# Attention with relative positions on one Trainium2 core: another DRAM layout for the position terms of the scores

## The chip, the core and the metric

The kernel runs on one core of a Trainium2 chip. The core has a matrix engine (TensorE; PE in the profile, with its weight loads shown as PEld), a vector engine (DVE), an activation engine (ACT), a general engine (POOL) and a synchronisation engine (SP), which here issues nearly all DMA transfers. Sixteen DMA engines move the data between DRAM (HBM) and the on-chip memory SBUF. The metric is the device time of one execution in microseconds (us); lower is better.

## What is computed

The reference is one transformer block over 16 sequences of 512 tokens with 256 channels, all in float32: a modulated layer normalisation, attention with 16 heads of 16 channels and relative positions, a second modulated normalisation, and a layer of 8 experts of which two count for each token. What matters here is the attention's scores:

```python
scores = jnp.einsum('bhqd,bhkd->bhqk', q, k)
dist_idx = pos_l - pos_r + M - 1
pos_emb = dist_emb[dist_idx]
rel_q = jnp.einsum('bhld,lrd->bhlr', q, pos_emb)
rel_k = jnp.einsum('bhrd,lrd->bhlr', k, pos_emb)
scores = (scores + rel_q + rel_k) / jnp.sqrt(jnp.asarray(D, scores.dtype))
probs = jax.nn.softmax(scores, axis=-1)
```

`rel_q + rel_k`, called the terms below, is a number for each batch, head, query position l and key position r: 16 x 16 x 512 x 512 values, 268 MB in all. The kernel works them out with (batch, head) on the 128 partitions, but the scores need l on the partitions. So the terms go through DRAM once: written in one arrangement, read back in the other. The change is about how they lie there.

## The kernel before, in words

**Tiles of the terms.** The 16 sequences are taken in two halves `s` of 8; 8 sequences times 16 heads are 128 rows, one for each partition. The 512 query positions are cut into four ranges `lb` of 128 and each of these into two of 64 (`lh`); the key positions into four ranges `rb` of 128 (`RK`). A block `n` (0 to 63) is one (s, lb, rb, lh): 128 rows x 64 l x 128 r, held in one of two buffers `two[n % 2]`. `q_set(n, g)` (line 156) makes 16 of its 64 l for all r with matrix products copied out by ACT (lines 165 and 175); `k_set(n, g)` (line 177) adds the second term for 32 of its 128 r and all 64 l, with products added in by DVE (lines 186 and 195). `store(n, g)` (line 199) writes 16 of the 64 l to DRAM: 1 MB. So all four `k_set` of a block must be done before its first store.

**In DRAM.** There are eight tensors `rel_d`, one for each (s, lb) (line 115). Each holds 128 rows (batch, head), 128 l and 512 r: 32 MB. Eight blocks, hence 32 stores, fill one.

**Reading back.** The main loop takes a unit `u` (0 to 63) = (s, lb, one sequence): 128 query positions of one sequence, 16 heads, in four groups `g` of four heads. `load_scores(u, g)` (line 577) brings the terms of four heads into a tile `st` of 128 l x 4 heads x 512 r, 1 MB; four such tiles exist (line 550). `content(u, g)` (line 637) multiplies queries and keys (line 644), and DVE adds the loaded terms and takes the maximum, one instruction for each head `t` (line 650). `exps` exponentiates (line 660), `turn` transposes the result on PE (line 669, out through lines 672 and 674), `context` multiplies with the values (line 687). The output projection, the second normalisation and the experts (lines 698 to 860) follow for the unit before.

**Two stages.** First a prologue: `prepare(b)` makes queries, keys and values of all 16 sequences and puts them in DRAM; `stationary(s)` loads them again as `raw` tiles, reorders and transposes them into the operands `e` of the blocks, and stores these (`e_d`); `blocks(n)` makes the first ten blocks (`LEAD = 10`, line 398), merged with the rest by hand. Then constants such as the experts' weights `we_sb` are loaded (line 558), and the main loop runs. It is written out by hand: each unit has 16 slots, and the table of lines 868 to 912 puts every step into a slot. With q0 = 16u + 4g:

- `load_scores(u, g)` in slot q0 - 12, `content(u, g)` in q0 - 4, `exps` in q0 - 2 and q0 - 1, `turn(u, g, t)` in q0 + t, `context(u, g)` in q0 + 5. The tile that a load fills is the one that `turn` of the group four before has last read, in slot q0 - 13.
- the four stores of block u + 10 in slots 16u + 28, 30, 32 and 34; its last `k_set` in slot 16u + 27.
- the other loads of a unit between them: keys `k` (line 590), queries `qs` (601), values `vu` (621), and `hbu`, `xu`, `gt`, `gf` for the later steps (628 to 634); the operands `qe` and `ke` of the next block (153); one store of the result (859).

The units 54 to 63 make no more blocks, since all 64 are done.

**Order.** Each engine runs its instructions in the order in which the program lists them. Nearly all DMAs stand in SP's one list: an SP instruction that waits holds back every DMA behind it. The framework gives the DMAs completion semaphores and the waits. The eight blocks of an `rel_d` tensor are all stored before the first unit that reads it; the last of these stores stands two slots ahead of that load.

Of the kernel before, what the change touches and what calls it, by code (L numbers as in the profile page):

```python
# [8 lines left out]
F32 = mybir.dt.float32  # L9
# [7 lines left out]
P = 128  # L17
E = 256
S = 512
# [10 lines left out]
RK = 128  # L30
# [4 lines left out]
def adaln_attention_moe_kernel(  # L35
# [34 lines left out]
    nc = tc.nc  # L70
    NB = x.shape[0]
    NL = S // P
# [8 lines left out]
    dram = ctx.enter_context(tc.tile_pool(name="dram", bufs=1, space=DRAM))  # L81
# [30 lines left out]
        for s in range(2)  # L112
    }

    rel_d = [dram.tile([P, P, S], F32, tag=f"rel_{n}", name=f"rel_d{n}") for n in range(8)]

    ps = ctx.enter_context(tc.tile_pool(name="ps", bufs=7, space=PSUM))
    ps_c = ctx.enter_context(tc.tile_pool(name="ps_c", bufs=1, space=PSUM))
# [7 lines left out]
    class Rel:  # L126
# [72 lines left out]
        def store(self, n, g):  # L199

            s, lb, rb, lh = self.at(n)
            l0 = lh * LQ + 16 * g
            nc.sync.dma_start(
                out=rel_d[s * 4 + lb][:, l0 : l0 + 16, rb * RK : (rb + 1) * RK],
                in_=self.two[n % 2][:, 16 * g : 16 * g + 16, :],
            )

# [3 lines left out]
    with ExitStack() as pro:  # L211
# [205 lines left out]
        with tc.tile_pool(name="setup", bufs=1) as su:  # L417
# [7 lines left out]
            for name, w in (("wq", wq), ("wk", wk), ("wv", wv)):  # L425
                nc.scalar.dma_start(
                    out=w_sb[name], in_=w.rearrange("(kc p) n -> p kc n", p=P)
# [78 lines left out]
            for t in range(4):  # L506
                for i in range(2):
                    rows = slice(32 * t + 16 * i, 32 * t + 16 * i + 16)
                    nc.sync.dma_start(
                        out=t_f[rows, i, i : 2 * S], in_=ext[:, 0 : 2 * S - i]  # L510
                    )
                    nc.sync.dma_start(
                        out=t_r[rows, i, i : 2 * S - 1], in_=rev[:, 0 : 2 * S - 1 - i]
# [4 lines left out]
                out=m8, in_=m8, compare_op=ALU.is_ge, fill=0.0,  # L518
# [3 lines left out]
                out=m8, in_=m8, compare_op=ALU.is_ge, fill=0.0,  # L522
# [7 lines left out]
        for cc in range(NE):  # L530
            for pa in range(2):
                for t in range(4):
                    row = cc * P + t * 32 + pa * D
                    nc.sync.dma_start(
                        out=wo_sb[pa * 64 + t * D : pa * 64 + (t + 1) * D, cc, :],
                        in_=wo[row : row + D, :],
# [34 lines left out]
    def place(u):  # L571
        s, lb, bb = u // 32, u % 32 // 8, u % 8
        return s, lb, bb, s * HB + bb
# [3 lines left out]
    def load_scores(u, g):  # L577

        s, lb, bb, b = place(u)
        h0 = bb * H + (g // 2) * 8 + g % 2  # L580
        st = sp.tile([P, 4, S], F32, tag="s", name=f"s_{u}_{g}")
        nc.sync.dma_start(
            out=st, in_=rel_d[s * 4 + lb][h0 : h0 + 7 : 2].rearrange("h l r -> l h r")
        )
        units[u]["s", g] = st

    def load_k(u, cc):
# [280 lines left out]
    for u in range(NP):  # L868
        z = 16 * u
        for g in range(4):  # L870
            q0 = z + 4 * g
            at(q0 - 12, 0, load_scores, u, g)
            at(q0 - 4, 5, content, u, g)
            at(q0 - 2, 7, exps, u, g, (0, 1))
            at(q0 - 1, 7, exps, u, g, (2, 3))
            for t in range(4):
                at(q0 + t, 3, turn, u, g, t, t > 0)
            at(q0 + 5, 4, context, u, g)
# [23 lines left out]
        n = u + LEAD  # L902
# [62 lines left out]
```

## Time and profile before

| | |
|---|---|
| Time, three runs | 2971.85, 2974.68, 2978.81 us (median 2974.68) |
| Profiled execution, its own time | 2971.56 us |
| Its span, first to last instruction | 2969.8 us |
| Mean granted TensorE clock | 0.971 |
| Terms written, DMAs | 256 of 1 MB, median 8.5 us from issue to landing |
| Terms read, DMAs | 256 of 1 MB, median 7.8 us from issue to landing |
| DRAM read, written in all | 462 MB, 328 MB |

The profile is a page of one execution and a trace that can be asked further. Its line of 40 slices shows each engine's busy share in tenths; each slice is 74 us, so the prologue is about the first six and a half, and the units without blocks are the last four. The chain of waits follows the end of the program back from releaser to releaser. The windows give busy time, granted clock and DMA share for any stretch. Columns are named where lines are shown.

### The profile page before, as it was taken

Reading aid. Unit: us, or ns where it says so; the run is one execution under the profiler, and the core shown is the slowest. Engines: PE = TensorE matmul, PEld = TensorE weight load, DVE = VectorE, ACT = ScalarE, POOL = GpSimd, SP = SyncE. Lnnn points to the kernel's source line nnn. Section 1 sums busy time; section 2 is a strip of 40 time slices with the busy share of each in tenths; the row PEclk is TensorE's granted clock in tenths of the full one; section 3 lists DMA queues with packets and bytes.
Section 4 is the critical chain, followed back from the end, with each engine's and each line's share of the span. In section 5 each row is a group of like instructions: output and inputs, shape, how many; then the busy total and the mean of one; then the engine's idle time right before and its main releaser. Section 6 shows DMA issues by size and latency. Waiting matters only on the chain.

```text
span 2969.8 us, 75984 instructions
## 1 busy us (share of the span) xinstructions
PE 2815.0 (95%) x30186; PEld 1845.8 (62%) x30186; DVE 1984.0 (67%) x5396; ACT 1933.7 (65%) x3682; POOL 629.8 (21%) x863
## 2 busy tenths in 40 slices
PE   8889864999999999999999999999999999999997
PEld 5556552666666666666666666666666666666564
DVE  5446542777777777777767777677777767776664
ACT  2344433777776777777677677777767777767774
POOL 1000000121222222122222212222222222222333
PEclk9889866999999999999999999999999999999999
DMA  6879997798988889988888998888898888898661
GB/s 191 302 260 319 298 302 259 229 290 268 287 269 271 280 283 293 280 272 281 272 271 277 287 281 274 268 283 277 281 295 268 286 273 272 272 280 279 211 232 54
DMA packets 855346, 796.46 MB, mean 268 GB/s; under 512 B 25545, under 2 KB 649409, under 8 KB 854737
## 3 DMA queue, kind: packets, MB, share of 16 engines
q1 hardware_dynamic: 854032, 790.03, 84.3%
q8 instruction: 240, 3.93, 0.5%
q10 hardware_dynamic: 960, 1.57, 0.2%
q14 instruction: 114, 0.93, 0.1%
HBM read 462.20 MB, written 328.25 MB: 266 GB/s over the span
## 4 chain that ended last, share of the span: by engine, by line
PE 79%; POOL 2%; DMA 1%; DVE 1%; SPq 1%; issue 1%; ACT 1%; POOLq 0%; ACTq 0%; DVEq 0%
PE pt L669 18%; PE fpy L830 14%; PE pq L165 13%; PE qk L644 12%; PE pc L687 8%; PE pk L186 8%; PE ph L735 2%; PE fpl L791 1%; PE pcl L702 1%; POOL qm L614 1%; DMA vu<-v_d 1%; PE fpt L778 1%; PE fpb L821 0%; PE pct L719 0%; POOL rstd L101 0%
## 5 line engine op out<-in xcount | busy, mean ns | idle before, releaser
L175 ACT COPY r<-pq 128x512 f32<-128x512 f32 x1024 | 525.4, 603 | 385.8 <-PE pq L165 368.9
L195 DVE TENSOR_TENSOR r<-pk,r 128x512 f32<-128x512 f32 x1024 | 635.0, 683 | 192.8 <-PE pk L186 187.3
L660 ACT ACTIVATE s<-s,mx 128x512 f32<-128x512 f32 x1024 | 691.6, 735 | 50.2 <-DVE mx L654 47.2
L650 DVE CUSTOM_DVE_ANT_0 s<-qk,s 128x512 f32<-128x512 f32 x1024 | 644.0, 685 | 39.2 <-PE qk L644 36.7
L669 PE MATMUL pt<-ident,s 128*128 128x128 f32 x4096 | 652.0, 283 | 10.7 <-ACT s L660 10.3
L669 PEld LDWEIGHTS pt<-ident,s 128*128 128x128 f32 x4096 | 451.0, 142 | 289.3 <-issue 77.7
L672 ACT COPY pT<-pt 128x512 f32<-128x512 f32 x768 | 459.5, 598 | 252.1 <-PE pt L669 250.4
L851 POOL TENSOR_TENSOR ye<-ye,ye 128x256 f32<-128x256 f32 x192 | 140.6, 732 | 1633.0 <-ACT ye L845 1627.5
L830 PE MATMUL fpy<-we_sb,fhT 128*128 128x512 f32 x1024 | 483.4, 595 | 0.0
L165 PE MATMUL pq<-t_r,qe 32*128 32x256 f32 x4096 | 467.1, 417 | 4.0 <-DMA qe<-eq_d 2.9
L644 PE MATMUL qk<-k,qm 32*128 32x512 f32 x2048 | 388.9, 644 | 28.0 <-POOL qm L614 28.0
L186 PEld LDWEIGHTS pk<-t_f,ke 32*128 32x128 f32 x8192 | 268.8, 190 | 189.1 <-ACT pT L672 157.7
L841 DVE SCALAR_TENSOR_TENSOR fy<-fpy,fmask,fy 128x256 f32<-128x256 f32 x256 | 123.8, 483 | 384.6 <-PE fpy L830 375.6
L165 PEld LDWEIGHTS pq<-t_r,qe 32*128 32x128 f32 x4096 | 283.3, 186 | 143.1 <-DVE mx L650 67.8
L186 PE MATMUL pk<-t_f,ke 32*128 32x128 f32 x8192 | 321.2, 288 | 7.2 <-DVE r L195 3.4
L687 PE MATMUL pc<-pT,vu 128*32 128x128 f32 x8192 | 278.2, 277 | 0.0
L830 PEld LDWEIGHTS fpy<-we_sb,fhT 128*128 128x128 f32 x1024 | 175.4, 191 | 124.9 <-issue 124.9
L687 PEld LDWEIGHTS pc<-pT,vu 128*32 128x32 f32 x8192 | 209.2, 110 | 43.5 <-issue 42.9
L644 PEld LDWEIGHTS qk<-k,qm 32*128 32x128 f32 x2048 | 141.5, 183 | 104.6 <-DVE r L195 47.3
L674 DVE COPY pT<-pt 128x512 f32<-128x512 f32 x256 | 174.5, 682 | 24.9 <-PE pt L669 20.3
L101 POOL TENSOR_TENSOR rstd<-rstd,mhalf 128x1 f32<-128x1 f32 (+1 forms) x144 | 88.0, 611 | 438.5 <-DVE rstd L100 434.9
L845 ACT ACTIVATE ye<-fpy,fmask 128x256 f32<-128x256 f32 x256 | 127.5, 498 | 45.2 <-DVE fy L841 45.1
(111 smaller groups left out, 2175.6 us busy)
## 6 DMA issues: line engine op xcount, KB each, us to landing
rel_d<-r SPq DMA_DIRECT2D x256, 1024.0 KB, 8.5
s<-rel_d SPq DMA_DIRECT2D x256, 1024.0 KB, 7.8
vu<-v_d SPq DMA_DIRECT2D x64, 576.0 KB, 7.7
ke<-ek_d SPq DMA_DIRECT2D x128, 256.0 KB, 7.1
k<-k_d SPq DMA_DIRECT2D x128, 256.0 KB, 6.5
gt<-gates_d SPq DMA_DIRECT2D x64, 256.0 KB, 4.7
v_d<-v SPq DMA_DIRECT2D x16, 576.0 KB, 6.4
xt<-in_x SPq DMA_DIRECT2D x16, 512.0 KB, 6.1
```

Of the source, the lines that this page charges most:

```text
L165: nc.tensor.matmul(bs[t][:, a * 256 : (a + 1) * 256], e[32 * t : 32 * t + 32, (g % 2) * 2 + a, :], t_r[32 * t : 32 * t + 32, :, m0 : m0 + RK],
L175: nc.scalar.copy(dst[:, t], bs[t].rearrange("p (a c) -> p a c", a=2))
L186: nc.tensor.matmul(bs[t][:, a * 128 : (a + 1) * 128], e[32 * t : 32 * t + 32, a, :], t_f[32 * t : 32 * t + 32, :, m0 : m0 + LQ], start=Tru ...
L195: nc.vector.tensor_tensor(dst, bs[t].rearrange("p (r l) -> p l r", r=8), dst, ALU.add)
L644: nc.tensor.matmul(bs[t], t_["q"][rows, pa, cc, :], t_["k", cc][rows, :], start=True, stop=True)
L650: nc.vector.tensor_tensor_reduce(st[:, t, :], bs[t], st[:, t, :], 0.25, -3.0e38, ALU.add, ALU.max, mx[:, t : t + 1],)
L660: nc.scalar.activation(t_["s", g][:, t, :], t_["s", g][:, t, :], AF.Exp, bias=t_["m", g][:, t : t + 1])
L669: nc.tensor.transpose(pt[:, cols], t_["s", g][:, t, cols], ident)
L672: nc.scalar.copy(pT, pt)
L674: nc.vector.tensor_copy(pT, pt)
L687: nc.tensor.matmul(pc[32 * t : 32 * t + 32, g, :], t_["v"][:, rb, h * VW : h * VW + 32], pTs[t][:, rb * P : (rb + 1) * P], start=(rb == 0) ...
L830: nc.tensor.matmul(py, t_["hT"][:, kc, :], we_sb[:, kc, pr * 2 * E : (pr + 1) * 2 * E], start=(kc == 0), stop=(kc == NE - 1),)
```

## The change

Before, a row (batch, head) of `rel_d` lies as [l, r]: 128 l of 512 r each. After, it lies as [r / 128, l, r % 128]: four slabs, one for each key range `rb`, each of 128 l of 128 r.

- The store of 16 l and one `rb` writes, for each partition, 16 runs of 512 bytes that lie 2 KB apart in DRAM before, and one run of 8 KB after. It stays one DMA of 1 MB.
- The load reads, for each l and head, one run of 2 KB before, and four runs of 512 bytes that lie 64 KB apart after. It is one DMA of 1 MB for four heads before, and four DMAs of 256 KB, one for each head, after. The tile in SBUF keeps its form.

No instruction of PE, DVE, ACT or POOL is added or removed by the diff, and no step changes its slot.

```diff
-    rel_d = [dram.tile([P, P, S], F32, tag=f"rel_{n}", name=f"rel_d{n}") for n in range(8)]
+    rel_d = [dram.tile([P, NL, P, RK], F32, tag=f"rel_{n}", name=f"rel_d{n}") for n in range(8)]
...
             nc.sync.dma_start(
-                out=rel_d[s * 4 + lb][:, l0 : l0 + 16, rb * RK : (rb + 1) * RK],
+                out=rel_d[s * 4 + lb][:, rb, l0 : l0 + 16, :],
                 in_=self.two[n % 2][:, 16 * g : 16 * g + 16, :],
             )
...
         st = sp.tile([P, 4, S], F32, tag="s", name=f"s_{u}_{g}")
-        nc.sync.dma_start(
-            out=st, in_=rel_d[s * 4 + lb][h0 : h0 + 7 : 2].rearrange("h l r -> l h r")
-        )
+        for t in range(4):
+            nc.sync.dma_start(
+                out=st[:, t, :].rearrange("p (rb r) -> p rb r", r=RK),
+                in_=rel_d[s * 4 + lb][h0 + 2 * t].rearrange("rb l r -> l rb r"),
+            )
```

## The prediction, made before the change was run

> **What bounds the kernel now.** I read the page first: busy times, the 40 slices, the DMA queues.
>
> ```profile
> PE 2815.0 (95%) x30186; PEld 1845.8 (62%) x30186; DVE 1984.0 (67%) x5396; ACT 1933.7 (65%) x3682; POOL 629.8 (21%) x863
> ...
> PE   8889864999999999999999999999999999999997
> ...
> DMA  6879997798988889988888998888898888898661
> ...
> DMA packets 855346, 796.46 MB, mean 268 GB/s; under 512 B 25545, under 2 KB 649409, under 8 KB 854737
> ...
> q1 hardware_dynamic: 854032, 790.03, 84.3%
> ```
>
> PE is full from slice 8 on; the DMA engines are not far behind. So I asked for windows by stage (window, its length, then busy time and instructions of PE, PEld, DVE, ACT, POOL; granted clock, DMA share, GB/s):
>
> ```profile
> 250.00:300.00 50.00, 47.85 (x489) 29.87 (x490) 34.60 (x76) 23.83 (x43) 2.01 (x2) 0.97 1.05 317
> 300.00:350.00 50.00, 48.59 (x525) 32.12 (x523) 27.47 (x49) 24.86 (x47) 0.14 (x1) 0.97 0.97 294
> 350.00:400.00 50.00, 35.01 (x347) 27.74 (x346) 24.21 (x72) 20.94 (x41) 0.00 (x0) 0.66 1.07 318
> 400.00:450.00 50.00, 29.02 (x272) 23.45 (x276) 18.95 (x40) 16.54 (x32) 0.00 (x0) 0.64 0.96 293
> 450.00:500.00 50.00, 13.38 (x102) 8.04 (x96) 12.01 (x28) 6.99 (x13) 2.64 (x3) 0.57 0.82 271
> ...
> 1000.00:1500.00 500.00, 500.00 (x5708) 327.26 (x5709) 356.56 (x957) 357.35 (x689) 116.40 (x160) 1.00 0.90 281
> ```
>
> Three regimes. From 560 to 2640 us PE has no gap, at full clock, and DMA is at 0.9. From 250 to 350 PE and DMA are both nearly full. From 350 to 490 DMA is full and PE is not. The chain of waits (start, duration, what) gives a unit's period in the main loop, 1230.75 - 1190.70 = 40.05 us, and the way through the transition:
>
> ```profile
> 476.96 8.00 DMA qs<-q_d
> 486.24 2.21 PE qk L644 x8
> ...
> 1190.70 1.84 PE qk L644 x8
> ...
> 1230.75 1.84 PE qk L644 x8
> ```
>
> The DMA queue's own timeline shows why `qs` lands late, at 485: four stores and 2 MB of expert weights are ahead of it. Its waits (total, times, longest) show what SP does in the main loop, and one wait that no data explains:
>
> ```profile
> 460.73 9.64 SPq L203 DMA_DIRECT2D rel_d<-r  x4
> 470.77 3.29 SPq L558 DMA_DIRECT2D we_sb<-in_we_t  x1
> ...
> SPq L203 <- DVE r L195: 516.2, 48, 11.6
> ...
> SPq L621 <- DMA we_sb<-in_we_t: 4.3, 1, 4.3
> ```
>
> L621 loads `vu` and has nothing to do with `we_sb`. Exactly eight DMAs start from `we_sb` up to it (`we_sb`, `wr_sb`, `be_sb`, `br_b`, `qs` twice, `k`, `s`), and the landings in the trace carry eight semaphores in turn: a DMA here waits until the one eight before it has landed. The first wait says that SP sits up to 11.6 us before a unit's first store, so it has slack.
>
> **What the Trainium skill says.** "DMA: Bandwidth & Descriptors", section Specifications, puts the least size for line rate at 512 B, and its section Why small descriptors are slow names a fixed cost for each packet. The trace agrees that a fixed part exists: its packet records, grouped by size, have means of 28.7 ns at 512 B (589,824 packets, most often 27), 96.9 at 2 KB (192,512, 84), 184 at 4.6 KB (178) and 334 at 8 KB (309; 375 packets). The section Rules for kernel authors asks for 1 MiB or more in a DMA; the loads go to 256 KB, and the trace has `k` at 256 KB landing in 6.5 us against 7.8 for 1 MB, which is queueing more than size. The section Latency and other measured facts lists power-of-two row pitches that slow HBM down from 2 MiB on, and not at 512 KiB; the stores step 256 KB from partition to partition before and after, so I take no loss. No run here shows it.
>
> **The change part by part.** All on the profiled execution, 2971.56 us (span 2969.8), 3.1 under the median of the runs.
>
> *Stores.* Before: 128 x 16 = 2,048 packets of 512 B, 2,048 x 28.7 / 16 engines = 3.67 us. After: 128 of 8 KB, 128 x 334 / 16 = 2.67. That is -1.0 us each. Bounds: pure stretches of stores in the main loop run at some 670 packets/us, 3.05 us, so -0.4; -1.2 with the quiet figures of 8 KB.
>
> *Loads.* Before: 512 packets of 2 KB, 3.10 us. After: 2,048 of 512 B, 3.67. That is +0.6. Bounds: most 512 B packets are writes; the `raw` loads near 150 us read 512 B runs at 30 ns and some 590 packets/us, 3.47 us, while 2 KB reads run at 195/us, 2.63; so up to +0.85.
>
> A pair thus costs between -0.4 and +0.45 us of DMA time; I take -0.3. A unit has four pairs, within 2 us either way, on 0.885 x 40.05 = 35.4 us of DMA work. It stays under 40.05, so the main loop keeps PE's period. Sum there: 0. The cover is 4.6 us of idle DMA a unit.
>
> *Latency of loads.* Three more issues at about 0.45 us (0.40 median of L582, plus the gap) and 0.6 more transfer: the last head lands 2 us later. The slots leave eight of 2.5 us, 20 us, from issue to use, landing takes 7.8; the landing records leave at least 6.9 us of margin in the main loop and mostly 5 to 11 in the last ten units, where a slot is 1.8 us. DVE needs head 0 first and 0.6 us for each, so head-by-head landing gives some back. Sum 0. Queued behind the four issues are `k`, `ke`, `vu`, `hbu`; they have 8 slots and more.
>
> *SP.* 12 more issues a unit, 5.4 us, against waits of up to 11.6 in the unit: hidden. The DMA behind a store is held 3 to 5 us now (`hbu` 5.5, `out_x` 5.1)[...]; that moves to the loads, which get four times the descriptors. Neutral, since data is moved in order either way. DVE's waits: three more semaphores a group, on an engine at 0.71; nothing.
>
> *Prologue, 213 to 460 us.* Only stores, 36 of the first 40: 36 us of DMA time gone. Up to 350 PE is full, so at most 3 us of it counts; I take 0. From 350 to 460, 12 stores give 12 us. The waits there that reach PE and begin with a DMA: 9.1 us at 407 (`ep_k` for `rot_k` for a late `raw_k`), 3.3 at 432 and 2.7 at 394 (for stores of `e`), 15 in all. The rest of PE's idle time is a ring of PE, DVE and ACT with some 7 us a turn, which no DMA shortens. I take a third, -5 (bounds 0 and -15).
>
> *Transition.* Four stores ahead of `qs`, 4 x -1.0 (bound -0.4): I take -3. Then the first load of scores: it landed at 488.33 and DVE used it at 488.46, so no margin, and by the rule of eight its heads 1 to 3 wait until `we_sb`, `wr_sb` and `be_sb` have landed, about 483. Head 0 is early, the others come 0.9 us apart against DVE's 0.6. I take +1 (0 to +4).
>
> *End of the blocks.* Near 2695 a load is waited for once, 2.5 us (the only wait of L650 for terms); slower loads lengthen it by 0 to 3, I take +1.
>
> Sum: -5 - 3 + 1 + 1 = -6: 2965.6 by the profiled execution, 2968.7 beside the median; I say 2968.
>
> **Rivals.** *Hidden anyway:* PE's ring alone sets 350 to 460 and the transition's gain goes to the later first load. For it: 7 us turns at 365 and 440 without a DMA wait. Against: `qs` at 485 is plainly behind DMA. Time: 2974 (0 to -2).
>
> *All of the prologue's DMA waits go:* -15 there, -3 up to 350, -4 in the transition, and a higher clock (0.65 granted while PE is idle): 2950. For it: SP is held after each store, and `raw_k` was issued behind such holds. Against: data order hardly changes.
>
> *Slower: the eight DMAs in flight.* A unit goes from 21 DMAs to 33. At a mean landing of 8 us SP needs 21 x 8 / 8 = 21 us a unit before, 33 after, of 40.05. It decides when the mean landing passes 9.7 us (33 x 9.7 / 8 = 40); each 0.1 us above costs 0.41 us a unit, over 54 units 22 us. At 9.8: 2997. For it: stores land at 8.5, single loads at 13.7. Against: with eight DMAs of at least 1.6 MB in flight the engines don't run dry, and landing times are mostly queue, which this limit itself shortens.
>
> **How the numbers follow.** The forecast, a gain of 2 to 20 us (2955 to 2973), has 0.58; hidden 0.15; all of it 0.07; slower 0.20. A measurement tells 0.2%, 5.9 us, from nothing. Of the forecast's case 0.40 lies beyond that and 0.18 within; with 0.07 of the large gain faster has 0.47, same 0.33 with the hidden case, slower 0.20. The range 2950 to 2990 leaves out half of the large gain and most of the slower case, 0.19; the likeliest case's own range is 2955 to 2973.
>
> **What would show it.** Packets near 757,000 in all, with 33,000 of 8 KB near 334 ns and 512 B still near 29; unit period 40.05; DMA share in the main loop 0.85 to 0.93; first `qk` of the main loop at 476 to 484 instead of 486.2; end of the four stores' issue well under 9.6 us; no wait of L650 for terms over 5 us. A unit period over 40.05, or waits of PE for DVE's L650 in every unit, would prove me wrong, as would an 8 KB packet well over 400 ns.

## The result, and the profile after

| | before | after |
|---|---|---|
| Median of 20 runs each, on the same chip | 2976.11 us | 2965.16 us |
| Lowest and highest | 2971.28, 2983.12 | 2960.49, 2970.65 |
| Profiled execution, its own time | 2971.56 us | 2963.32 us |
| Its span | 2969.8 us | 2961.6 us |

The ratio is 0.9964, with a 95% interval from 0.9956 to 0.9972: 10.7 us less, from 8.3 to 13.1. The forecast was 2968, a gain of 6 us over the runs known then; the measured gain is nearly twice that.

The page of the kernel after, the lines that answer to those of before (busy times, slices of PE and DMA, packets, the main DMA queue):

```profile
PE 2817.5 (95%) x30186; PEld 1844.4 (62%) x30186; DVE 1984.2 (67%) x5396; ACT 1932.1 (65%) x3682; POOL 628.2 (21%) x863
...
PE   8779865999999999999999999999999999999997
...
DMA  6878887889988888898888989888889898888681
...
DMA packets 769344, 796.64 MB, mean 269 GB/s; under 512 B 37833, under 2 KB 661697, under 8 KB 735953
...
q1 hardware_dynamic: 768016, 790.07, 83.8%
```

The engines do the same work. The DMA queue fell from 84.3% of 2969.8 us to 83.8% of 2961.6: 2503.5 to 2481.8 us, or 0.085 us for each of the 256 pairs of a store and a load. Over the whole kernel the change thus saves next to no DMA time. The gain has to come from where stores outweigh loads, and the windows by stage of the kernel after point there (window, length, then busy time and instructions of PE, PEld, DVE, ACT, POOL; granted clock, DMA share, GB/s):

```profile
250.00:300.00 50.00, 47.69 (x528) 30.71 (x528) 35.05 (x77) 24.50 (x44) 2.01 (x2) 1.00 0.76 292
300.00:350.00 50.00, 48.58 (x523) 31.63 (x522) 28.93 (x51) 25.01 (x47) 0.14 (x1) 0.98 0.86 312
350.00:400.00 50.00, 33.37 (x348) 26.21 (x347) 24.44 (x74) 21.74 (x43) 0.00 (x0) 0.84 0.94 342
400.00:450.00 50.00, 33.18 (x320) 26.64 (x320) 22.47 (x45) 16.82 (x32) 0.00 (x0) 0.64 0.77 272
450.00:500.00 50.00, 20.76 (x190) 12.04 (x191) 14.07 (x41) 15.83 (x29) 3.65 (x4) 0.66 0.93 303
1000.00:1500.00 500.00, 500.00 (x5706) 326.95 (x5705) 357.57 (x959) 356.99 (x687) 119.99 (x165) 1.00 0.87 276
```

Read the DMA share down the rows. It is the sum of the packets' times over 16 engines, so it passes 1 where packets overlap. In the prologue it fell by 0.1 to 0.3 (at 400 to 450 us from 0.96 to 0.77), where nothing but stores of terms changed. PE did 320 matmuls from 400 to 450 us instead of 272, and 190 instead of 102 in the next row, since the main loop starts sooner. In the last row PE is full as before, 500 of 500 us, with DMA at 0.90 before and 0.87 after.

The chain of waits of the kernel after (start, duration, what), through the transition and over one unit of the main loop:

```profile
449.95 1.21 DVE r L195 x2
...
452.97 10.96 DMA rel_d<-r
...
463.95 7.66 DMA s<-rel_d
...
471.63 2.13 PE qk L646 x8
...
695.41 1.84 PE qk L646 x8
...
735.46 1.84 PE qk L646 x8
```

The period is 735.46 - 695.41 = 40.05 us, as before. The first `qk` comes 14.6 us sooner. Two of the chain's steps need care. `s<-rel_d` is named as what released `qk`, but `qk` reads `k` and `qm`, and POOL makes `qm` from `qs`: the DMAs share eight semaphores, and the name here is that of another one landing then. And the first load of scores begins at 463.95, the moment the store issued eight DMAs before has landed: the rule of eight that the prediction read off `vu`, on another line.

The DMA queue's timeline of the kernel after (start, duration, what) shows the change most plainly. The same four stores took 9.64 us to issue before:

```profile
451.17 3.06 SPq L203 DMA_DIRECT2D rel_d<-r  x4
454.64 0.90 SPq L558 DMA_DIRECT2D we_sb<-in_we_t  x1
...
463.95 6.47 SPq L583 DMA_DIRECT2D s<-rel_d  x4
```

The hold of SP has gone over from the stores to the loads of scores, where the main loop covers it.

### The profile page after: what moved, and what is told of

The parts are those of the page before. It is cut to its first block, busy times and chain, and to the rows that moved or that the text cites. A ratio compares the mean times of both kernels' runs of the same rounds, so it can differ in the third digit from the quotient of the medians.

```text
span 2961.6 us, 78018 instructions
## 1 busy us (share of the span) xinstructions
PE 2817.5 (95%) x30186; PEld 1844.4 (62%) x30186; DVE 1984.2 (67%) x5396; ACT 1932.1 (65%) x3682; POOL 628.2 (21%) x863
## 3 DMA queue, kind: packets, MB, share of 16 engines
q1 hardware_dynamic: 768016, 790.07, 83.8%
## 4 chain that ended last, share of the span: by engine, by line
PE 78%; DMA 2%; POOL 2%; ACT 1%; DVE 1%; issue 0%; SPq 0%; POOLq 0%; ACTq 0%; DVEq 0%
PE pt L671 17%; PE fpy L832 14%; PE pq L165 13%; PE qk L646 12%; PE pc L689 8%; PE pk L186 8%; PE ph L737 2%; DMA s<-rel_d 1%; PE fpl L793 1%; PE pcl L704 1%; POOL qm L616 1%; PE fpt L780 1%; PE fpb L823 0%; PE pct L721 0%; DMA vu<-v_d 0%
## 5 line engine op out<-in xcount | busy, mean ns | idle before, releaser
L671 PE MATMUL pt<-ident,s 128*128 128x128 f32 x4096 | 653.2, 283 | 10.6 <-ACT s L662 10.2
```

Source lines behind the costliest of these rows:

```text
L671: nc.tensor.transpose(pt[:, cols], t_["s", g][:, t, cols], ident)
```

## The experiments

The theory at the start: in the prologue and the transition, a store as 128 packets of 8 KB takes less DMA time than as 2,048 of 512 bytes; all gain comes from the first 40 stores, and the main loop hides both directions. The expectations call this theory A or A1. Its rivals: that the gain has another source (loads cut by head, B; runs that lie together in DRAM, A2; stores in the main loop, F; the hold of SP behind a store, G), and that the slower loads cost something that hides part of the gain (D). Theory E is the other reading of the program's end: that TensorE's clock, and not the loads, takes time there.

Five marks in each profile say where a kernel differs: the last block of the prologue (start of DVE's 160th pass of line 195), the first `qk` of the main loop, the first matmul of the experts (`fpy`), the period of a unit, and the last way, from DVE's last pass of line 195 to the end. Each row is one profile, in us from the start of the span; line numbers of other kernels can differ by a few.

| kernel | last block of the prologue | first qk | first fpy | period | last way |
|---|---|---|---|---|---|
| before | 460.0 | 486.2 | 564.9 | 40.05 | 301.2 |
| after | 450.5 | 471.6 | 550.2 | 40.05 | 307.6 |
| after, run again | 457.1 | 478.2 | 556.8 | 40.05 | 307.5 |
| only the loads cut | 463.9 | 489.4 | 570.5 | 40.05 | 309.6 |
| new layout, first two tensors | 457.6 | 478.7 | 557.3 | 40.05 | 304.9 |
| new layout, other six | 460.2 | 487.2 | 568.3 | 40.05 | 307.7 |
| new layout, small packets | 457.8 | 483.6 | 562.5 | 40.05 | 307.0 |
| mask early, after | 455.0 | 476.1 | 557.2 | 40.07 | 307.2 |
| mask early, before | 463.5 | 489.3 | 570.1 | 40.07 | 306.6 |
| stores on POOL's queue | 473.6 | 487.6 | 571.9 | 40.05 | 307.5 |
| more bytes in the prologue | 528.2 | 561.5 | 640.3 | 40.06 | 300.7 |
| modulate later, after | 453.7 | 474.8 | 556.1 | 40.41 | 296.1 |
| modulate later, before | 464.7 | 490.7 | 569.5 | 40.41 | 299.9 |
| modulate later at the end, after | 454.0 | 475.2 | 553.8 | 40.05 | 297.0 |

**Only the loads cut.** The layout of before, with four loads of 256 KB in runs of 2 KB.

```diff
-        nc.sync.dma_start(
-            out=st, in_=rel_d[s * 4 + lb][h0 : h0 + 7 : 2].rearrange("h l r -> l h r")
-        )
+        for t in range(4):
+            nc.sync.dma_start(out=st[:, t, :], in_=rel_d[s * 4 + lb][h0 + 2 * t])
```

> The old layout, and only the loads cut into four, head by head (256 KB each, runs of 2 KB). Theory A (the gain is the stores' shorter DMA time before the main loop, nothing else of the change matters): the first qk of the main loop stays at 483 to 489 us, the unit period at 40.05, the ratio to before within 0.998 to 1.002. Rival B (heads landing one by one make the gain): first qk near 472, ratio near 0.9964. Rival C (33 DMAs a unit instead of 21, under the rule of eight, cost time somewhere): ratio over 1.002.

Measured: 2974.95 against 2978.38, ratio 0.9992 (0.9983 to 1.0001); the period stays at 40.05. The DMA queue's timeline of this kernel has the stores' issue as before:

```profile
464.65 9.65 SPq L203 DMA_DIRECT2D rel_d<-r  x4
```

So loads head by head neither bring the gain nor cost anything that the runs show, and with 768 more DMAs the limit of eight in flight doesn't lengthen a unit. Both fall as rivals.

**Small packets in the new layout.** The block's buffer gets two unused columns, so that each run of 128 r stands alone in SBUF. A store still fills 8 KB in one piece in DRAM for each partition, but in packets of 512 bytes.

```diff
-            self.two = [rblk.tile([P, LQ, RK], F32, name=f"r_{i}") for i in range(2)]
+            self.two = [rblk.tile([P, LQ, RK + 2], F32, name=f"r_{i}")[:, :, 0:RK] for i in range(2)]
...
-                "p (a t i) r -> p t a (i r)", a=2, t=4
+                "p (a t i) r -> p t a i r", a=2, t=4
...
-                nc.scalar.copy(dst[:, t], bs[t].rearrange("p (a c) -> p a c", a=2))
+                nc.scalar.copy(dst[:, t], bs[t].rearrange("p (a i r) -> p a i r", a=2, i=2))
```

> The changed kernel, but each row of 128 in the block buffers is followed by two unused elements, so that the store has to be cut into packets of 512 bytes although it still fills 8 KB in one piece in DRAM. Theory A1 (what counts is the number of packets of the store): the gain is gone, first qk of the main loop at 483 to 489 us, ratio to before 0.998 to 1.003; DMA share in the main loop 0.93 to 0.97. Rival A2 (what counts is that the bytes lie in one piece in DRAM): first qk near 472, ratio near 0.9964.

Measured: 2978.42, ratio 1.0003 (0.9995 to 1.0012): the whole gain is gone. The page of this kernel, packets and the main queue:

```profile
DMA packets 1260863, 796.64 MB, mean 268 GB/s; under 512 B 37832, under 2 KB 1185984, under 8 KB 1260240
...
q1 hardware_dynamic: 1259536, 790.07, 90.2%
```

Its timeline of the DMA queue, and its windows:

```profile
458.48 9.63 SPq L203 DMA_DIRECT2D rel_d<-r  x4
```

```profile
350.00:400.00 50.00, 32.60 (x348) 25.44 (x341) 25.54 (x74) 20.29 (x40) 0.00 (x0) 0.84 1.09 326
...
1000.00:1500.00 500.00, 500.00 (x5712) 327.09 (x5702) 356.40 (x958) 356.81 (x687) 114.28 (x158) 1.00 0.97 281
```

Thus it is the packet that counts and not how the bytes lie in DRAM. The gaps in the buffer don't slow the engines that fill it: ACT's copy (line 175) takes 606 ns against 604 in after, DVE's pass (line 195) 683 in both. This is also the worst case for the main loop, with small packets in both directions: DMA at 0.97, and PE still without a gap.

**New layout for some tensors.** First for the two that the prologue fills, then for the other six alone.

```diff
-    rel_d = [dram.tile([P, P, S], F32, tag=f"rel_{n}", name=f"rel_d{n}") for n in range(8)]
+    NEW = (0, 1)
+    rel_d = [
+        dram.tile([P, NL, P, RK] if n in NEW else [P, P, S], F32, tag=f"rel_{n}", name=f"rel_d{n}")
+        for n in range(8)
+    ]
...
+            d = rel_d[s * 4 + lb]
...
-                out=rel_d[s * 4 + lb][:, l0 : l0 + 16, rb * RK : (rb + 1) * RK],
+                out=(
+                    d[:, rb, l0 : l0 + 16, :] if s * 4 + lb in NEW
+                    else d[:, l0 : l0 + 16, rb * RK : (rb + 1) * RK]
+                ),
...
```

The second kernel has `NEW = range(2, 8)`. The loads follow their tensor's layout.

> The new layout and loads only for the two tensors of terms that are stored before the main loop (s 0, lb 0 and 1); the old layout and the 1 MB loads for the other six. Theory A: the whole gain up to the main loop, first qk at 470 to 475 us, ratio 0.9950 to 0.9975. The last ten units then have the old loads: if those of the changed kernel lose their 6 us to slower loads (rival D), this run keeps them and reaches 0.995; if they lose them to TensorE's clock, which falls to half for 3.4 us at a time wherever PE's pauses happen to fall (theory E), such half-clock stretches appear here too, in a number of 1 to 6 that differs from run to run.

> The reverse: the new layout and loads for the six tensors that are stored in the main loop, the old for the first two. Theory A: nothing gained, first qk of the main loop at 483 to 489 us, unit period 40.05, ratio 0.998 to 1.002. Rival F (the shorter stores help in the main loop or at its end as well): ratio under 0.998.

Measured: first two 2966.16, ratio 0.9961 (0.9947 to 0.9975); other six 2976.07, ratio 0.9995 (0.9985 to 1.0005). The gain sits in the first two tensors, and the main loop gains and loses nothing that the runs show. Two stretches at half clock lie in the last way of the kernel with the first two, as E had it. Only the mark was missed: the first `qk` came at 478.7, later than expected, as the prologue ended later than in the one profile of after. Its stores' issue, in the DMA queue's timeline of the kernel with the first two:

```profile
458.31 3.07 SPq L208 DMA_DIRECT2D rel_d<-r  x4
```

**Stores on POOL's queue.** Before, with its first 40 stores issued by POOL, so that SP isn't held.

```diff
-            nc.sync.dma_start(
+            q = nc.gpsimd if n < 10 else nc.sync
+            q.dma_start(
```

> The kernel before, its first 40 stores (blocks 0 to 9) issued by POOL's queue instead of SP's; same layout and same 512-byte packets. Theory A1 (the DMA time of 40 x 1 us is what was saved): first qk of the main loop at 483 to 492 us. Rival G (what was saved is that SP's queue is held 3 us behind each store, not the DMA time): first qk at 470 to 478.

Measured, one run: 2984.75, with the last block of the prologue at 473.6. The DMA issues on this kernel's page (count, KB, median us to landing):

```profile
s<-rel_d SPq DMA_DIRECT2D x256, 1024.0 KB, 7.9
rel_d<-r SPq DMA_DIRECT2D x216, 1024.0 KB, 8.3
rel_d<-r POOLq DMA_DIRECT2D x40, 1024.0 KB, 14.4
```

The first `qk` came at 487.6, where A1 had it, but this isn't a clean test of G. Stores from POOL take 14.4 us to land, and SP's other DMAs run beside them instead of behind: the last block came 13.6 us later than in before, and the way from it to the first `qk` took 14.0 us instead of 26.2, since `qs` no longer stands behind four stores. Nor are the packets the same: the trace has each store from POOL as 256 packets of 4 KB with a mean of 213 ns, 3.4 us of DMA time.

**More bytes in the prologue.** After, with a second store behind each of the first 40, of 48 of the partitions, into a buffer that nobody reads. This adds work; nothing is left out.

```diff
+    extra_d = dram.tile([40, 48, 16, RK], F32, name="extra_d")
...
+            if n < 10:
+                nc.sync.dma_start(
+                    out=extra_d[n * 4 + g], in_=self.two[n % 2][0:48, 16 * g : 16 * g + 16, :]
+                )
```

> The changed kernel, with a second DMA behind each of the 40 stores made before the main loop: 48 of the 128 partitions once more, in 8 KB runs, into a buffer that nobody reads. That is 48 x 334 / 16 = 1.0 us of DMA time for each store, as much as the change saves there, but only 3 descriptors for each DMA engine, so SP's queue is not held for it. Theory A1 (the stores' DMA time): the gain before the main loop is gone, first qk at 483 to 490 us, ratio to before 0.998 to 1.003. Rival G (the hold of SP's queue behind a store of 2,048 descriptors): first qk at 471 to 479, ratio near 0.997.

Measured: 3050.6, ratio 1.0241 (1.0227 to 1.0256); the first `qk` came 90 us later than in after. Neither forecast was met. The dose was larger than meant: the packets of 8 KB before 560 us took 181 us of the sixteen engines instead of 118, which is 1.56 us for each of the 40. And each extra store keeps its block's buffer, as one of ACT's waits in this kernel says (total, times, longest):

```profile
ACT r L177 <- DMA extra_d<-r: 32.6, 11, 5.3
```

62 us of DMA time were added and 90 us lost. As the buffers were held as well, the run gives no price for one microsecond of DMA time.

**DMA time or SP's hold.** No run takes one away without the other. The traces of before and after speak for the DMA time. These are the kernel before's windows of the two stretches where most of the gain arises, the wait for a late `raw_k` near 407 us and the last four stores:

```profile
376.00:414.00 38.00, 24.42 (x238) 19.53 (x239) 16.89 (x62) 14.38 (x28) 0.00 (x0) 0.63 1.07 329
462.00:476.00 14.00, 0.00 (x0) 0.00 (x0) 0.00 (x0) 0.00 (x0) 0.00 (x0) 0.50 1.04 281
```

The chain of waits of before does run through SP's issues from 460.73 to 476.96 us, but while SP was held the DMA engines had no gap: the share is 1.07 and 1.04. In the second stretch they moved 266 to 294 GB/s in every microsecond but two, whether SP was held (to 470) or not (after it). The packets of the last four stores took 15.74 us of the sixteen engines before and 11.08 after; that is 4.7 of the 4.9 us which the way to the first `qk` is shorter on the mean of the profiles. So what SP's hold can have added there is small.

**The end of the program.** After's profile gained 14.6 us up to the last block of all (2668.6 to 2654.0), but 8.2 in its span. The rest is in the last way, 307.6 against 301.2. The suspicion was that the slower loads (D) cost something in the units without blocks. A second run of the kernel after, unchanged, was to show it:

> The changed kernel once more, unaltered. Theory E: the half-clock stretches between 2680 and 2930 us, five in the first profile of it, come in another number (1 to 6), each worth about 1.6 us of PE; the way from the last block to the end moves by that much. Rival D: the same five units lose the same time.

Measured: one run, 2969.74, a last way of 307.5, and again five stretches at half clock, in the same five units. That is what D had said; the other number that E expected did not come, so this run doesn't separate the two. The table of marks does. Kernels that read runs of 2 KB at the end have 301.2, 304.9, 306.6, 307.5 and 309.6 (before, first two, mask early on before, POOL, only the loads cut; mean 306.0), and those that read runs of 512 bytes 300.7, 307.0, 307.2, 307.5, 307.6 and 307.7 (mean 306.3). And the kernel with the new layout in the other six tensors, whose last units have the slower loads too, is at 0.9995 of before, at most 1.0005: 1.5 us. So a cost of 6 us (D) falls; the 301.2 of before is at the low end. What differs is the clock. Windows of the kernel before, across one of PE's pauses:

```profile
2724.00:2728.00 4.00, 2.15 (x19) 1.38 (x17) 2.47 (x9) 2.51 (x5) 2.57 (x4) 1.00 0.51 165
2728.00:2732.00 4.00, 4.00 (x52) 2.75 (x48) 3.47 (x16) 3.04 (x7) 0.10 (x1) 1.00 0.67 237
```

and of the kernel after, across another:

```profile
2708.00:2712.00 4.00, 2.17 (x10) 1.13 (x9) 3.07 (x12) 1.73 (x3) 3.17 (x5) 1.00 1.12 308
2712.00:2716.00 4.00, 4.00 (x38) 2.35 (x40) 2.83 (x9) 3.46 (x7) 0.73 (x1) 0.67 1.08 299
```

The pauses are alike, 2.15 and 2.17 us of PE in 4, but after the second the granted clock is 0.67 and PE gets through 38 matmuls instead of 52. PE's timelines show the same, before and then after (in brackets the idle time ahead and its releaser):

```profile
2726.45 0.44 PE L778 MATMUL fpt<-ident,xn 128*128 128x128 f32 x2 [1.85 <-DVE xn L768]
...
2727.25 1.22 PE L644 MATMUL qk<-k,qm 32*128 32x512 f32 x8
```

```profile
2770.26 0.44 PE L780 MATMUL fpt<-ident,xn 128*128 128x128 f32 x2 [1.82 <-DVE xn L770]
...
2771.06 2.01 PE L646 MATMUL qk<-k,qm 32*128 32x512 f32 x8
```

Eight `qk` take 1.22 us at full clock and 2.01 at half. The clock's records have such stretches of 3.4 us: one in before's last way, five in after's, beside two longer ones at the very end of both. Four more stretches go with 6.4 us more, 1.6 us each; 3.4 us at half clock can cost 1.7. "TensorE: Matmul & The Clock Gate" in the Trainium skill, section What's actually happening, describes a free-running window of 3413 ns and half the clock after at least one idle window. The traces agree on the window: in each of the fourteen profiles all changes of the clock lie on one grid of 3.413 us, to within 0.2% of a step. On the idle window they differ, since a pause of 1.8 us is enough here.

The grid also tells most of the equal pauses apart. A pause of 1.84 us that falls whole into one step leaves PE busy for 0.46 of it; one that is split over two steps leaves both busier. For all steps of the fourteen profiles from the last block's end to 30 us before the end, with PE's busy share and the clock of the step after:

| PE busy in a step | steps | followed by half clock |
|---|---|---|
| under 0.475 | 45 | 30 |
| 0.475 to 0.8 | 122 | 8 |
| over 0.8 | 954 | 0 |

Why the other 15 of the 45 were not followed by half clock is open. In the two runs of after the grid lies alike, 0.17 of a step from the last block's end, so that the clock, too, gives the same five units.

**Taking the pause away.** PE waits there at `fpt` for `xn`, the second normalisation. The first try moved the masking of queries two slots forward, to take it out of POOL's way.

```diff
-        at(z - 7, 0, mask_q, u)
+        at(z - 9, 0, mask_q, u)
```

> The changed kernel with mask_q two slots earlier (slot 16u - 9 instead of 16u - 7), so that POOL's two instructions of 0.92 us no longer stand between the residual and the second normalisation, for which PE waits 1.8 us in each unit without blocks. Theory E (the last ten units lose time to these pauses, and to half clock after them): 1.8 us for each of ten units and the half-clock stretches between 2690 and 2930 us go, 20 to 25 us in all: end of the last block's sums to the end of the span 260 to 266 us instead of 284; ratio to before 0.987 to 0.990. Rival D (slower loads hold the last units): the units keep 28.5 to 30 us, ratio stays near 0.996.

> The kernel before with the same move of mask_q. Theories A and E together: it gains 18 to 22 us over before, ratio 0.992 to 0.9945, and the changed kernel with the move is 13 to 15 us faster than this one, since nothing is left that gives the prologue's 14.7 us back. Rival D: the difference stays at 11 or less.

Measured: on after 2967.49, ratio 0.9969 (0.9958 to 0.9981), last way 307.2; on before 2982.06, ratio 1.0014 (1.0007 to 1.0021), last way 306.6. The last way didn't shorten, so both missed; only the distance of the two kernels, 14.6 us, is the one expected (13 to 15; D: 11 or less). The 284 us in the expectation aren't the table's last way, which is 307.6 in after. The chain of waits of the second shows why nothing was gained:

```profile
2757.90 0.58 POOL rstd L101
...
2759.52 0.60 DVE s L650
...
2762.16 0.34 DVE stats L763
...
2763.56 0.42 DVE xn L768
```

POOL is done at 2758.48, but DVE first runs its four additions of the scores (line 650) before it turns to `stats`: the order in DVE's own list, not POOL, makes `xn` late.

**Modulate later.** So PE's side was moved instead: `fpt` one slot later.

```diff
-        at(z + 11, 6, modulate, u)
+        at(z + 12, 6, modulate, u)
```

> The changed kernel with modulate one slot later (16u + 12 after the unit instead of 11). In e7 the pause of PE before it stayed although POOL was free, with DVE's four instructions of the next scores between the residual and the second normalisation; so here PE gets a slot of other work instead of the wait. Theory E: the pauses of 1.8 us in ten units and most half-clock stretches go, the way from the last block's sums to the end of the span falls from 307 to 280 to 292 us, ratio to before 0.987 to 0.992. Otherwise it stays near 0.996.

> The kernel before with the same move of modulate. Theory E: ratio to before 0.991 to 0.996, the same way to the end falls to 280 to 292 us. Theory A: the changed kernel with the move is 10 to 14 us faster than this one.

Measured: on after 2975.89, ratio 0.9991 (0.9984 to 0.9997); on before 2993.38, ratio 1.0048 (1.0034 to 1.0062). Both ratios missed. The last way is shorter, 296.1 and 299.9, though not 280 to 292, and the period rose from 40.05 to 40.41: over 54 units 0.36 us cost 19. The two kernels lie 17.5 us apart, more than the 10 to 14 expected. PE shows no wait in it, and why PE's work takes longer in that order is open. The last kernel keeps the old order while there are blocks:

```diff
-        at(z + 11, 6, modulate, u)
+        at(z + (12 if u >= 53 else 11), 6, modulate, u)
```

> The changed kernel with modulate one slot later for the units from 53 on alone. In e10 the move for all units shortened the way from the last block's sums to the end of the span to 296 us (307.5 in e8), and lengthened the unit period from 40.05 to 40.41, some 19 us in all. Here the period is to stay at 40.05 and the end to keep the gain: first qk at 471 to 479, last way 294 to 301 us, time 6 to 12 us below the changed kernel, ratio to before 0.992 to 0.9945. If the longer period was not the price of the move in the main loop, or the shorter end came from chance in the clock alone, the ratio stays at 0.996.

Measured: 2959.81, ratio 0.9935 (0.9921 to 0.9950), below the whole interval of after, with all marks where they were expected. PE's waits from 2650 to 2960 us in after (total, times, longest), and then in this kernel:

```profile
PE fpt L780 <- DVE xn L770: 21.9, 11, 5.1
```

```profile
PE pt L671 <- ACT s L662: 6.5, 9, 0.7
PE fpt L780 <- DVE xn L770: 5.5, 2, 5.1
```

and the windows of the last units in after, then in this kernel with its main loop beside them:

```profile
2657.00:2947.00 290.00, 264.74 (x2468) 168.93 (x2468) 179.00 (x574) 191.55 (x366) 91.32 (x127) 0.96 0.68 198
```

```profile
2660.00:2950.00 290.00, 267.71 (x2484) 168.06 (x2484) 180.14 (x578) 193.70 (x371) 96.91 (x135) 0.99 0.69 199
1000.00:1500.00 500.00, 500.00 (x5708) 327.47 (x5708) 357.52 (x962) 355.73 (x685) 120.14 (x165) 1.00 0.88 277
```

Nine of the eleven long waits are gone, with nine short ones for `pt` in their place. None of the 3.4 us stretches at half clock is left, the clock is 0.99, and the last way 297.0. Of the 10.6 us to after, five stretches are 8 by the price above; PE's idle time in the window fell by 3.0, from 25.3 to 22.3.

## Why the prediction was right, and where its sizes were off

The forecast held: faster, by a little, from the prologue and the transition, with the main loop neutral. Its mechanism was right, its size little more than half: -6 against -10.7 us. One profile carries several microseconds of chance (the last block of the prologue lies at 450.5 in one run of after and at 457.1 in another), so the terms are measured on the marks of twelve profiles: six kernels that store 512-byte packets in the prologue (before, only loads cut, other six, small packets, mask early on before, modulate later on before) against six that store 8 KB (the two runs of after, first two, mask early, modulate later twice). The POOL kernel and the one with more bytes stay out.

- *A store costs 1.0 us less, a load 0.6 more.* Packets of 8 KB took 354 ns over the kernel, 322 up to 560 us: 2.83 and 2.58 us a store instead of 3.67. Loads of 512 bytes: 2,048 x 29.5 / 16 = 3.78 us instead of 3.10. A pair comes to -0.16 from the packets, and -0.085 from the queue's total; -0.3 was taken, -0.4 to 0.45 allowed (with the bound of -1.2 for a store the lower end is -0.6). The skill's fixed cost for each packet ("DMA: Bandwidth & Descriptors", Why small descriptors are slow) is what the small-packet kernel bears out: same bytes, same DRAM places, no gain, since sixteen packets of 512 bytes take 16 x 28.6 = 458 ns there against 354 for one of 8 KB.
- *Packets near 757,000.* There were 769,344. The count forgot that a DMA also sends 16 packets of 4 bytes, one for each engine: 768 x 16 = 12,288 more.
- *Main loop 0.* Right: the period is 40.05 to 40.07 us in all kernels but the two with modulate later throughout. Cover for DMA remained even at a share of 0.97.
- *SP's 12 more issues hidden.* Right, though they cost more than 5.4 us: from 600 to 2600 us, 50 units, the loads held SP for 622 us instead of 245, 7.5 us more a unit. But all DMA issues together took 1328 us instead of 1299, since other DMAs are held less. That is the "neutral" of the prediction.
- *Latency of loads covered.* Right: DVE's waits in after have no line for terms. Loads land 6.1 us after issue, against 7.8.
- *Prologue -5 (0 to -15).* Too small: the last block comes at 461.7 on average with small packets and at 454.7 with large ones, -7.0. Most of the chance lies earlier: from DVE's 128th pass of line 195 to its 160th the six of one kind take 83.6 to 85.7 us and the six of the other 76.7 to 78.4, means 84.7 and 77.8. And it comes where the prediction looked: PE's longest wait for `rot_k`, the 9.1 us at 407, is 8.3 to 10.9 in the one kind and 4.7 to 5.6 in the other. But the third of 15 us that was taken was a guess, and came near by luck.
- *Transition -3.* Too small, and the best measured term: from last block to first `qk` 25.5 to 27.0 us in the six of one kind, 21.1 or 21.2 in all six of the other; the means are 26.0 and 21.1, -4.9. The last of the four stores landed 17.6 us after the first issue before and 12.8 in after: -1.2 us a store, at the far bound. The step took three quarters of a DMA time of 1.0 us a store; the packets of these four stores show 1.2 (15.7 to 11.1 us), and all of it counted. SP's hold, which fell from 9.64 to 3.06 us and isn't in the step, isn't needed for the sum.
- *First load of scores +1.* Not seen. Heads 1 to 3 did wait for `we_sb` and its neighbours, as the rule of eight had it: they were issued from 468.95 us on, when `we_sb` had landed at 468.93. But DVE's first pass of scores begins 2.1 us after the first `qk`, 2.2 before, and the next three follow at 0.6. From first `qk` to first `fpy` the means are 79.9 and 79.4, with values near 78.7 and 81.1 in both kinds.
- *End of the blocks +1.* Nothing seen: the last ways of the two kinds of loads have means of 306.0 and 306.3, and the wait of 2.5 us for terms in before is not in after.
- *Not foreseen:* the half clock in the last way. It doesn't belong to the change, but a profile of one execution can have 6 us of it, and did.

The three terms at the start come to -12.4 us by these means, against a gain of 10.7 (8.3 to 13.1) measured. The three rivals fall: hidden anyway, by the ratio; all DMA waits of the prologue gone, by -7.0 out of 15; eight in flight, by the kernel with only the loads cut and the period of 40.05. The sign for the first `qk`, 476 to 484, was passed in after's profile (471.6) and just missed by the mean (475.8).

## What to carry to other kernels

A layout that makes one direction of a DMA cheap and the other dear is worth judging stage by stage: here the sum over the kernel was nearly nought, and the time came from the one stage where the cheap direction ran alone and DMA set the pace. What the cheap direction saves there can be read from its packets' times, as in the last four stores. Count packets by the shortest run on either side, since a contiguous target with a broken source gained nothing. And before a few microseconds between two profiles are explained, compare several kernels by marks along the program: here the same kernel's prologue differed by 6.6 us between two runs.

## What the runs showed of the hardware that was not expected

- TensorE's clock can fall to half for 3.4 us after a pause of only 1.8 us, in one to five of the last ten units, and not after the same pause in others; each stretch cost some 1.6 us. The changes lie on a grid of 3.413 us, and what counts most is whether a pause falls whole into one step: half clock followed 30 of the 45 steps with PE busy for under 0.475, and 8 of the 1076 others.
- Moving one small step of PE by a slot lengthened every unit by 0.36 us, with PE full and no wait shown.
- Four stores in a row of 2,048 packets hold the issuing queue for 9.6 us, of 128 packets for 3.1, although the DMA time of the small packets is only 1.3 to 1.4 times that of the large; the small-packet kernel, with the new layout, has 9.6 again.
- The DMA engines' share can stand at 0.97 for 500 us without one gap on PE, where the slots leave 20 us from a load's issue to its use.
